# Layer 3's neighbour slots laid out slot by slot and gathered without the empty ones, with edits of layer 1's order, in a four-layer graph network

## The chip, the cores and the metric

The kernel runs on one core of a Trainium2 chip. The metric is the device time of one execution, in microseconds; the numbers of one profiled execution come from the hardware profiler. PE is the matrix engine, DVE the vector engine, ACT the scalar engine, POOL the GpSimd engine, which also issues the indirect DMAs (gathers and scatters of rows by index), and SP the engine that issues most plain DMAs.

## The reference

There are N = 2708 nodes with D = 128 features, and an adjacency matrix of 2708 x 2708 float32 in which about 17 entries a row are not zero (the diagonal is always there). Four layers follow one another, each of the form x = layernorm(x + f(x, adj)):

```
layer 0: f = (adj^T x) / column sums of adj
layer 1: s = x Wa^T, d = x Wb^T;  agg[i] = sum_j adj[i,j] * gelu(s[i] + d[j] + b)
         f = layernorm(gelu([x, agg] U^T + c) + x)
layer 2: h = adj (x W) + b;  f = leaky_relu(batchnorm over nodes (h))
layer 3: for each of 4 heads: x1 = x w1, x2 = x w2
         score[i,j] = exp(8 tanh((leaky_relu(x1[i] + x2[j]) . a) / 8)) * adj[i,j]
         out = leaky_relu((score / row sum) x Wlin^T);  f = concat(heads) w
```

## The kernel before, in words

The adjacency is used as lists. In layer 0 the kernel loads the rows in 22 blocks of 128 nodes. PE makes the column sums and adj^T x (L453), POOL clears the diagonal (L443, an affine select a block) and DVE extracts the positions and values of the non-zero entries (L478 to L521, the extraction of a block). Nodes are then ranked by the number of their neighbours, in two groups (the first SPLIT = 13 blocks and the other 9), and the lists are scattered to memory in that order. `caps` holds, for each block and each 32 nodes, how many neighbours the written tables allow (QUARTERS); where data exceed them a flag sends the program to a dense path, which doesn't run here. Before the extraction there is a little set-up of index patterns by DVE (L700 to L716) from three POOL iotas (L693 to L697). The `caps` memsets (L415) are written ahead of them.

In layer 1 each block of 128 ranked nodes takes its neighbours slot by slot: one gather per slot from `d_dram` (L263, tile msg) into a ring, issued by `gather_spaced`, which puts three short `pause` memsets (L280) on POOL behind every fourth gather. DVE adds the own term `s_ps` (made by PE at L924 to L927 from x_s), ACT does the gelu, DVE weighs and sums (L938, `parts`), PE forms the update (L968 to L979), a normalisation follows, and PE transposes the result (L997) for its row write to `x2_dram`. Other work is put beside the blocks: `layer2(k)`, a gather of 128 rows of the transposed adjacency (`at_rows`) into a ring and one set of matrix products into six standing accumulators (L1076, with a column sum at L1067); lists for layer 3 (L675); and the 13 gathers `x2_first` of layer 2's rows from `x2_dram[0]`, which need all 13 row writes of the first group. A tile scheduler orders the instructions of each engine from the order of writing and its own estimate. Layer 3 is written with a manual order on PE, DVE, ACT and POOL.

In layer 2 the rest of the batch normalisation is done, and for each node a row of 644 floats is written to `t2_dram` (its x2 terms of four heads, its features and padding). Tables for layer 3 (`masks`, iotas at L1170 and L1172) are built in between.

In layer 3 the nodes stand in 24 blocks, `BLOCKS3`, given as (g, j): a chunk holds g nodes with c = 128 // g slots each, e = g c rows, and one index a row. Four chunks make a quad, one from each quarter of the block, j quads a block, 100 quads in all:

```
BLOCKS3 = [
    *[(4, 8), (5, 6), (6, 5), (6, 5), (6, 5), (7, 4), (7, 4), (7, 4), (8, 4), (8, 4), (8, 4)],
    *[(9, 3), (9, 3), (10, 3)],
    *[(4, 3), (5, 5), (6, 4), (6, 5), (7, 3), (7, 4), (8, 4), (8, 4), (9, 3), (10, 3)],
]
```

 `fetch(i)` issues the four gathers of a quad (L263, tile g) into a set of the pool `got`, which rotates over GOT = 9 sets. PE's `repeated` adds up the own terms of the chunk's nodes, and for two chunks the gathered rows (L1463, L1469, tile z); DVE adds the own terms for the other two (L1663), takes leaky relu times a (`scores` L1479, `products` L1487); ACT sums the products over the features (L1495); PE divides out sums and forms the weighted sum of the gathered features (L1540, tile po_s). DVE wrote sums and products into the set of the gathered rows itself. The closing work of a quad is queued and done some quads later. Output rows are scattered from POOL (L284). POOL's order in layer 3 is fetch by fetch with the pauses between, so that the next fetch is issued as soon as a set is free.

Of the kernel before, what the change touches and what calls it, by code (L numbers as in the profile page):

```python
# [9 lines left out]
FP = mybir.dt.float32  # L10
AF = mybir.ActivationFunctionType
ALU = mybir.AluOpType
# [46 lines left out]
]  # L59
KINDS = sorted({g for g, _ in BLOCKS3})  # L60
# [29 lines left out]
GOT = 9  # L90
# [4 lines left out]
def gnn_resnorm_kernel(  # L95
# [155 lines left out]
    wrong3 = keep.tile([P, NB3], FP, name="wrong3")  # L251
# [116 lines left out]
    with ExitStack() as layer:  # L368
# [44 lines left out]
        for b in range(NBLK):  # L413
            for q, most in enumerate(QUARTERS[b]):
                nc.gpsimd.memset(caps[32 * q : 32 * q + 32, b : b + 1], float(most))  # L415
# [52 lines left out]
        def extract(b, rows):  # L468
# [21 lines left out]
            junk = small.tile([P, CAND], FP, name="junk_c")  # L490
# [171 lines left out]
        def spread(b, po, c0):  # L662

            g, j = BLOCKS3[b]
            c, q = P // g, 4 * j
            e = g * c
            for i, k0 in enumerate((0, SLOTS)):
                part = mine.tile([P, g, c], FP, name=f"spread{g}", tag="spread", bufs=2)
                nc.vector.tensor_tensor(
                    part,  # L670
                    lists3[:, b % 6, k0 : k0 + c].unsqueeze(1).to_broadcast((P, g, c)),
                    of_row[g].unsqueeze(2).to_broadcast((P, g, c)),
                    ALU.mult,
                )
                nc.tensor.matmul(  # L675
                    po[0:e, c0 + i * q : c0 + (i + 1) * q],
                    lhsT=part.rearrange("p g c -> p (g c)"),
                    rhs=of_chunk[g][:, 0:j, :].rearrange("p j r -> p (j r)"),
                    start=True, stop=True,
                )  # L680
            at = slice(CHUNK3[b], CHUNK3[b + 1])
            nc.vector.tensor_copy(val3[0:e, at], po[0:e, c0 : c0 + q])
            nc.vector.tensor_copy(idx3[0:e, at], po[0:e, c0 + q : c0 + 2 * q])
            nc.vector.tensor_copy(to3[:, b : b + 1], node3[:, b, 1:2])
            n, bad = 4 * g * j, wrong3[:, b : b + 1]
            nc.vector.tensor_scalar(bad[0:n], node3[0:n, b, 0:1], float(c - 1), None, ALU.is_gt)
            nc.vector.scalar_tensor_tensor(
                bad[0:n], node3[0:n, b, 0:1], 1.0, bad[0:n], ALU.is_lt, ALU.add
            )
# [14 lines left out]
        of_row, of_chunk = {}, {}  # L704
# [48 lines left out]
        nc.scalar.dma_start(w2_l2, l2_w)  # L753
        for b in range(SPLIT):
# [164 lines left out]
        def messages(b, x_s, three):  # L919
# [7 lines left out]
            nc.tensor.matmul(  # L927
                s_ps[0:n], lhsT=ones[0:1, 0:n], rhs=msgb[0:1, :], start=False, stop=True
            )
            parts = mine.tile([P, 2, D], FP, name="parts")  # L930
# [161 lines left out]
        for i, b in enumerate(TURNS):  # L1092
# [9 lines left out]
            x_st, agg = messages(b, x_s, three)  # L1102
# [22 lines left out]
            if i >= 11:  # L1125
                for k in range(2 * (i - 11), min(i, 2 * (i - 10))):
                    layer2(k)
            if i > SPLIT:
                if i == SPLIT + 1:
                    x2_first = late.tile([P, SPLIT, D], FP, name="x2_first", tag="late")  # L1130
                for b in range(2 * (i - SPLIT - 1), min(SPLIT, 2 * (i - SPLIT))):
# [26 lines left out]
    with ExitStack() as layer:  # L1158
# [6 lines left out]
        def masks(g):  # L1165
# [4 lines left out]
            nc.gpsimd.iota(row_of, pattern=[[1, g], [0, c]], base=0, channel_multiplier=0)  # L1170
            start = small.tile([P, g], I32, name=f"start{g}", tag="start", bufs=2)
            nc.gpsimd.iota(start, pattern=[[-c, g]], base=0, channel_multiplier=1)  # L1172
# [16 lines left out]
            after = small.tile([P, g], FP, name=f"after{g}", tag="after", bufs=2)  # L1189
            count = small.tile([P, 1], FP, name="count", bufs=2)  # L1190
            nc.vector.tensor_scalar(
                after, start, 0.0, None, ALU.is_ge, ALU.add, accum_out=count
            )
            mask[g] = ready.tile([P, g], FP, name=f"mask{g}")
            nc.vector.scalar_tensor_tensor(
                mask[g], start, float(c), after, ALU.is_lt, ALU.mult
# [157 lines left out]
    with ExitStack() as layer:  # L1354
        work = layer.enter_context(tc.tile_pool(name="s3", bufs=1, reuse_waits="tile"))
        mine = layer.enter_context(tc.tile_pool(name="s3_mine", bufs=2, reuse_waits="tile"))
        got = layer.enter_context(tc.tile_pool(name="s3_got", bufs=GOT, reuse_waits="tile"))
# [117 lines left out]
        def scores(e, r, z, a, g4, sc):  # L1475

            for hd in range(HEADS):
                part_of = slice(hd * D, (hd + 1) * D)
                nc.vector.scalar_tensor_tensor(  # L1479
                    g4[0:e, r, part_of], z[0:e, part_of], 0.0, a[0:e, part_of],  # L1480
# [3 lines left out]
        def products(e, g4):  # L1484

            z = g4[0:e, 0:2, 0:HD]
# [4 lines left out]
        def sums_of_products(e, g4, sc, chunks):  # L1491
            for r in chunks:
                for hd in range(HEADS):
                    product = g4[0:e, r, hd * D : (hd + 1) * D]
# [139 lines left out]

        def fetch(i):
            b, j = quads[i]
            e = BLOCKS3[b][0] * (P // BLOCKS3[b][0])
            g4 = got.tile([P, 4, RW], FP, name="g4")
            for r in range(4):
                ch = CHUNK3[b] + 4 * j + r  # L1640
                gather_spaced(g4[0:e, r, :], t2_dram, idx3[0:e, ch : ch + 1])
# [4 lines left out]
        for i, (b, j) in enumerate(quads):  # L1646
# [11 lines left out]
            if i + 1 < len(quads):  # L1658
# [3 lines left out]
            z, a_row = g4[0:e, 0:2, 0:HD], a_99.rearrange("p h d -> p (h d)")  # L1662
            nc.vector.tensor_tensor(z, z, z2[0:e], ALU.add)  # L1663
            nc.vector.scalar_tensor_tensor(
                g4[0:e, 2, 0:HD], zs[0][0:e], 0.0, a_row[0:e], ALU.max, ALU.mult
            )
            scores(e, 3, zs[1], a_row, g4, sc4[:, 3, :])
            step()
            sums_of_products(e, g4, sc4, (2,))
# [4 lines left out]
            products(e, g4)  # L1674
            step()
            sums_of_products(e, g4, sc4, (0, 1))
# [531 lines left out]
```

## Time and profile before

| | us |
|---|---|
| median of 3 runs (lowest to highest) | 1655.01 (1653.0 to 1659.47) |
| the profiled execution | 1660.39 |
| its span | 1658.7 |
| mean granted TensorE clock | 0.755 |

In the lines shown below, a group line gives the source line, the engine, the operation, out<-in, the count, then busy time and mean duration in ns, and behind the second bar the idle time just before these instructions with what ended most of it. A line of the windows gives start and end, the length, the busy time of PE, of its weight loads (PEld), of DVE, ACT and POOL, each with its count, the granted clock, the share of the DMA engines and GB/s. A line of the waits gives the engine, the tile and line that waited, what ended the wait, the sum, the count and the longest. A line of the timeline gives start, duration, engine, line, operation and, in brackets, the idle time before it and what ended it. The stages by window: extraction to 208, layer 1 to about 863, layer 2 to 959, layer 3's quads to 1620, and the last blocks' closing to 1659.

### The profile page before, as it was taken

What the parts mean: (1) busy time and instruction counts of PE and PEld (TensorE: products, weight loads), DVE (VectorE), ACT (ScalarE), POOL (GpSimd) and SP (SyncE); (2) the same over time, 40 slices, a digit from 0 to 9 for tenths busy, and PEclk for the clock granted to TensorE, in tenths of its full rate; (3) what the DMA queues carried; (4) which work ended last, traced back from release to release, by engine and by line L of the source; (5) the groups of instructions that cost most, each with busy time, mean ns of one, the idle gap of its engine ahead of it and who ended that gap; (6) DMA issues with size and microseconds to landing.
All of it is one profiled execution on the core that took longest, in us unless ns stands there. A gap on an engine that the chain in (4) does not pass through costs nothing. (4 is left out here: it accounts for less than half of the span.)

```text
span 1658.7 us, 23258 instructions
## 1 busy us (share of the span) xinstructions
PE 1164.1 (70%) x5179; PEld 735.5 (44%) x5179; DVE 1093.4 (66%) x4560; ACT 811.9 (49%) x3491; POOL 1045.7 (63%) x1656
## 2 busy tenths in 40 slices
PE   7976434566248667353576778988889788898985
PEld 6976323445136433131333324544444445454444
DVE  6999767888435452264465555877768777587874
ACT  2638467755134210021122545776658666576763
POOL 2001487777776626777762577777777777777772
PEclk9998555555555578676566877999889999788996
DMA  8633367879546744811111576777677676676761
GB/s 277 260 135 132 90 171 226 240 213 259 135 103 174 252 172 153 314 52 48 41 42 35 202 204 189 200 212 204 190 202 219 192 199 187 191 208 188 216 190 39
DMA packets 163651, 288.42 MB, mean 174 GB/s; under 512 B 46786, under 2 KB 118514, under 8 KB 156401
## 3 DMA queue, kind: packets, MB, share of 16 engines
q0 software_dynamic: 60208, 189.68, 39.4%
q1 hardware_dynamic: 98053, 93.97, 18.4%
q10 hardware_dynamic: 5240, 3.18, 0.8%
q8 instruction: 44, 0.72, 0.2%
q14 instruction: 106, 0.87, 0.2%
HBM read 241.22 MB, written 45.45 MB: 173 GB/s over the span
## 5 line engine op out<-in xcount | busy, mean ns | idle before, releaser
L263 POOL DMA_INDIRECT g<-t_dram,idx x400 | 400.0, 1000 | 149.0 <-issue 105.7
L263 POOL DMA_INDIRECT msg<-d_dram,idx x368 | 347.9, 945 | 132.6 <-issue 78.7
L1495 ACT ACTIVATE g<-g 126x128 f32<-126x128 f32 (+3 forms) x1200 | 352.9, 297 | 65.7 <-DVE g L1487 25.7
L1469 PE MATMUL z<-g,ident 126*126 126x512 f32 (+3 forms) x400 | 245.4, 734 | 69.6 <-DMA g<-t_dram,idx 60.2
L1495 ACT ACTIVATION_READ_ACCUMULATOR g<-g 126x1 f32 (+3 forms) x1200 | 226.0, 188 | 3.6 <-issue 3.3
L1029 PE MATMUL pt_a<-ident,rows 128*128 128x128 f32 (+2 forms) x475 | 119.5, 411 | 118.8 <-ACT at_sb L1034 62.4
L1469 PEld LDWEIGHTS z<-g,ident 126*126 126x126 f32 (+3 forms) x400 | 73.8, 213 | 229.0 <-DMA g<-t_dram,idx 151.7
L1463 PE MATMUL z<-x,copies 32*126 32x512 f32 (+3 forms) x800 | 160.8, 686 | 7.8 <-DVE g L1663 4.8
L280 POOL MEMSET pause<- 1x200 int8 x591 | 150.5, 255 | 20.7
L453 PE MATMUL acc<-x_nat,rows 128*128 128x129 f32 (+3 forms) x1012 | 132.2, 293 | 30.5 <-DMA rows<-in_adj_dram 19.4
L1029 PEld LDWEIGHTS pt_a<-ident,rows 128*128 128x128 f32 (+2 forms) x475 | 84.4, 210 | 146.8 <-ACT at_sb L1034 76.1
L1663 DVE TENSOR_TENSOR g<-g,z 126x1024 f32<-126x1024 f32 (+3 forms) x100 | 121.7, 1217 | 41.8 <-PE z L1463 21.5
L1076 PE MATMUL acc<-at_rows,x_nat 128*128 128x512 f32 (+2 forms) x264 | 139.4, 676 | 13.4 <-DMA at_rows<-at_dram,perm 13.4
L453 PEld LDWEIGHTS acc<-x_nat,rows 128*128 128x128 f32 (+2 forms) x1012 | 126.1, 202 | 36.2 <-DMA rows<-in_adj_dram 20.7
L1487 DVE SCALAR_TENSOR_TENSOR g<-g,a_ps 126x1024 f32<-126x1024 f32 (+3 forms) x100 | 121.2, 1212 | 0.0
L938 DVE SCALAR_TENSOR_TENSOR own<-msg,ls,own 128x128 f32<-128x128 f32 (+1 forms) x302 | 105.4, 349 | 20.6 <-ACT msg L957 10.5
L957 ACT ACTIVATE msg<-msg 128x896 f32<-128x896 f32 (+4 forms) x55 | 50.4, 916 | 137.7 <-DVE msg L954 68.6
L1479 DVE SCALAR_TENSOR_TENSOR g<-z,a 126x128 f32<-126x128 f32 (+3 forms) x400 | 91.9, 285 | 35.0 <-PE z L1469 31.0
L1540 PEld LDWEIGHTS po_s<-wm,g 126*128 126x128 f32 (+3 forms) x800 | 105.3, 208 | 17.4 <-issue 12.3
L954 DVE TENSOR_TENSOR msg<-msg,own 128x896 f32<-128x896 f32 (+4 forms) x55 | 57.4, 1043 | 79.8 <-DMA msg<-d_dram,idx 76.1
L1540 PE MATMUL po_s<-wm,g 126*128 126x24 f32 (+6 forms) x800 | 103.4, 280 | 1.4 <-DVE wm L1527 0.9
L478 DVE FIND_INDEX8 ci<-cv,rows 128x8 uint32<-128x247 f32 (+2 forms) x242 | 98.5, 407 | 0.0
(319 smaller groups left out, 2058.2 us busy)
## 6 DMA issues: line engine op xcount, KB each, us to landing
rows<-in_adj_dram SPq DMA_DIRECT2D x34, 1354.0 KB
at_dram<-at_sb SPq DMA_DIRECT2D x105, 256.0 KB
t_dram<-t_row SPq DMA_DIRECT2D x10, 644.0 KB
g<-t_dram,idx POOLq DMA_INDIRECT x400
msg<-d_dram,idx POOLq DMA_INDIRECT x368
x_s<-dx_dram SPq DMA_DIRECT2D x21, 128.0 KB
at_dram<-at_sb SPq DMA_DIRECT2D x21, 64.0 KB
x_dram<-x_n SPq DMA_DIRECT2D x21, 64.0 KB
```

Of the source, the lines that this page charges most:

```text
L263: return nc.gpsimd.indirect_dma_start(out=dst, out_offset=None, in_=table[0 : min(N, table.shape[0]), :], in_offset=bass.IndirectOffsetOnA ...
L280: did = nc.gpsimd.memset(pause, 0)
L453: nc.tensor.matmul(accs0[k][0:m, c0 : c0 + f1 - f0], lhsT=rows[0:n, j0 : j0 + m], rhs=x_nat[0:n, b, f0:f1], start=k not in started, stop=( ...
L938: nc.vector.scalar_tensor_tensor(to, m, v, last, ALU.mult, ALU.add)
L1029: nc.tensor.transpose(pt[0:m, j, 0:n], rows[0:n, c0 : c0 + m], ident[0:n, 0:n])
L1076: nc.tensor.matmul(accs2[c][:, 0:cw], lhsT=xw[0:n, b, :], rhs=at[0:n, c0 : c0 + cw], start=(k == 0), stop=(k == NBLK - 1),)
L1463: nc.tensor.matmul(z2[0:e, r, :] if r < 2 else zs[r - 2][0:e], lhsT=copies[g][rows, j, :], rhs=own[b][1][rows, :], start=True, stop=r < 2, ...
L1469: nc.tensor.matmul(zs[r - 2][0:e], lhsT=ident[0:e, 0:e], rhs=g4[0:e, r, 0:HD], start=False, stop=True, skip_group_check=True,)
L1487: nc.vector.scalar_tensor_tensor(z, z, 0.0, a_ps[0:e].unsqueeze(1).to_broadcast((e, 2, HD)), ALU.max, ALU.mult)
L1495: nc.scalar.activation(product, product, AF.Identity, accum_out=sc[0:e, r, hd : hd + 1])
L1540: nc.tensor.matmul(po[:, p0 * HEADS : (p0 + g) * HEADS], lhsT=g4s[i][0:e, r, HD : HD + D], rhs=wm[0:e, 4 * i + r, :, :], start=True, stop= ...
L1663: nc.vector.tensor_tensor(z, z, z2[0:e], ALU.add)
```

## The change

- `QUARTERS3` says, for each block of layer 3 and each of the four chunks of a quad, how many slots the fullest node may have. The rows of a chunk are laid slot by slot (all g nodes' first slot, then all second ones) in place of node by node, in `spread`, the index patterns and the `masks`. So the empty slots lie at the end, and `fetch` gathers only the first m = g * QUARTERS3[b][r] rows from quad 8 on; the first eight quads gather all e rows, so that every set has been filled once.
- The lists are held against these caps (`caps3`, `wrong3`, `of_block`). The memsets of `caps` are written after the iotas, in fewer pieces, and those of `caps3` with them. In POOL's order the first affine select then comes before these memsets (46 of 128 rows, 81 of 32) and the second one after them.
- Layer 3's sums and products go into a tile of their own, `made`, with two buffers.
- GOT is 8, as eight tiles given out once. A gather then waits for its index and for PE, where the first gather of a quad waited for DVE, DMA, PE and ACT.
- In layer 1 the 13 `x2_first` gathers are written from turn 16 on, three a turn, where it was turn 14 and two. Two `layer2` sets are put behind the own term of the next block on PE, where they stood at the end of a turn; the last block takes three (18, 19 and 20), and set 21 comes at the end as before.

```diff
 ]
+QUARTERS3 = [
+    (31, 26, 25, 24), (23, 22, 22, 22), (21, 21, 21, 20), (20, 20, 20, 19),
+    (19, 19, 19, 19), (18, 18, 18, 18), (18, 17, 17, 17), (17, 17, 16, 16),
+    (16, 16, 16, 16), (15, 15, 15, 15), (14, 14, 14, 14), (14, 13, 13, 13),
+    (13, 12, 12, 12), (11, 11, 10, 9), (30, 26, 24, 24), (23, 23, 22, 21),
+    (21, 21, 20, 20), (20, 19, 19, 19), (18, 18, 18, 18), (17, 17, 17, 16),
+    (16, 16, 16, 15), (15, 15, 14, 14), (14, 13, 13, 13), (12, 12, 11, 9),
+]
 KINDS = sorted({g for g, _ in BLOCKS3})
...
 TOGETHER3 = [(0, 4), (4, 8), (8, 12), (12, 16), (16, 20), (20, 23), (23, 24)]
-GOT = 9
+GOT = 8
 LEAD3 = 5
...
 caps = work.tile([P, NBLK], FP, name="caps")
-for b in range(NBLK):
-    for q, most in enumerate(QUARTERS[b]):
-        nc.gpsimd.memset(caps[32 * q : 32 * q + 32, b : b + 1], float(most))
+caps3 = work.tile([P, NB3], FP, name="caps3")
...
 for i, k0 in enumerate((0, SLOTS)):
-    part = mine.tile([P, g, c], FP, name=f"spread{g}", tag="spread", bufs=2)
+    part = mine.tile([P, c, g], FP, name=f"spread{g}", tag="spread", bufs=2)
     nc.vector.tensor_tensor(
         part,
-        lists3[:, b % 6, k0 : k0 + c].unsqueeze(1).to_broadcast((P, g, c)),
-        of_row[g].unsqueeze(2).to_broadcast((P, g, c)),
+        lists3[:, b % 6, k0 : k0 + c].unsqueeze(2).to_broadcast((P, c, g)),
+        of_row[g].unsqueeze(1).to_broadcast((P, c, g)),
         ALU.mult,
...
 po[0:e, c0 + i * q : c0 + (i + 1) * q],
-lhsT=part.rearrange("p g c -> p (g c)"),
+lhsT=part.rearrange("p c g -> p (c g)"),
 rhs=of_chunk[g][:, 0:j, :].rearrange("p j r -> p (j r)"),
...
 nc.vector.tensor_copy(to3[:, b : b + 1], node3[:, b, 1:2])
-n, bad = 4 * g * j, wrong3[:, b : b + 1]
-nc.vector.tensor_scalar(bad[0:n], node3[0:n, b, 0:1], float(c - 1), None, ALU.is_gt)
+n = 4 * g * j
+nc.vector.tensor_scalar(
+    wrong3[0:n, b : b + 1], node3[0:n, b, 0:1], 1.0, None, ALU.is_lt
+)
 nc.vector.scalar_tensor_tensor(
-    bad[0:n], node3[0:n, b, 0:1], 1.0, bad[0:n], ALU.is_lt, ALU.add
+    wrong3[:, NB3 + b : NB3 + b + 1], lists3[:, b % 6, 2 * SLOTS : 2 * SLOTS + 1],
+    caps3[:, b : b + 1], of_block[g * j], ALU.is_gt, ALU.mult,
 )
...
 nc.vector.tensor_copy(in32, row_i)
-of_row, of_chunk = {}, {}
+of_row, of_chunk, of_block = {}, {}, {}
+spans = sorted({g * j for g, j in BLOCKS3})
+of_blocks3 = work.tile([P, len(spans)], FP, name="of_blocks3")
+for i, e in enumerate(spans):
+    of_block[e] = of_blocks3[:, i : i + 1]
+    nc.vector.tensor_scalar(of_block[e], in32, float(e), None, ALU.is_lt)
 for g in KINDS:
...
 nc.scalar.dma_start(w2_l2, l2_w)
+for b in range(NBLK):
+    for q, most in enumerate(QUARTERS[b]):
+        if not q or most != QUARTERS[b][0]:
+            at = slice(32 * q, 32 * q + 32) if q else slice(0, P)
+            nc.gpsimd.memset(caps[at, b : b + 1], float(most))
+for b in range(NB3):
+    for q, most in enumerate(QUARTERS3[b]):
+        if not q or most != QUARTERS3[b][0]:
+            at = slice(32 * q, 32 * q + 32) if q else slice(0, P)
+            nc.gpsimd.memset(caps3[at, b : b + 1], float(most - 1))
 for b in range(SPLIT):
...
-def messages(b, x_s, three):
+def messages(b, x_s, three, beside):
     n, kk = BLOCKS[b][1], CAPS[b]
...
 nc.tensor.matmul(s_ps[0:n], lhsT=x_st[:, 0:n], rhs=ws_t, start=True, stop=False)
-nc.tensor.matmul(
+term = nc.tensor.matmul(
     s_ps[0:n], lhsT=ones[0:1, 0:n], rhs=msgb[0:1, :], start=False, stop=True
 )
+for k in beside:
+    with tc.issue_after(term.ins):
+        layer2(k)
 parts = mine.tile([P, 2, D], FP, name="parts")
...
     load3(b3)
-x_st, agg = messages(b, x_s, three)
+x_st, agg = messages(
+    b, x_s, three,
+    range(2 * (i - 12), 2 * (i - 11) if i + 1 < NBLK else i) if i > 11 else (),
+)
 for _ in range(2 if i < 1 else 1):
...
     accs2.extend(banks("acc2_"))
-if i >= 11:
-    for k in range(2 * (i - 11), min(i, 2 * (i - 10))):
-        layer2(k)
-if i > SPLIT:
-    if i == SPLIT + 1:
+if i > SPLIT + 2:
+    if i == SPLIT + 3:
         x2_first = late.tile([P, SPLIT, D], FP, name="x2_first", tag="late")
-    for b in range(2 * (i - SPLIT - 1), min(SPLIT, 2 * (i - SPLIT))):
+    for b in range(3 * (i - SPLIT - 3), min(SPLIT, 3 * (i - SPLIT - 2))):
         gather_spaced(x2_first[:, b, :], x2_dram[0], rank[:, b : b + 1])
...
 row_of = small.tile([P, e], I32, name=f"row_of{g}", tag="row_of", bufs=2)
-nc.gpsimd.iota(row_of, pattern=[[1, g], [0, c]], base=0, channel_multiplier=0)
-start = small.tile([P, g], I32, name=f"start{g}", tag="start", bufs=2)
-nc.gpsimd.iota(start, pattern=[[-c, g]], base=0, channel_multiplier=1)
+nc.gpsimd.iota(row_of, pattern=[[0, c], [1, g]], base=0, channel_multiplier=0)
+apart = small.tile([P, c, g], I32, name=f"apart{g}", tag="apart", bufs=2)
+nc.gpsimd.iota(apart, pattern=[[-g, c], [-1, g]], base=0, channel_multiplier=1)
 first = small.tile([P, 8], FP, name="first", bufs=2)
...
 nc.vector.tensor_scalar(alike[g], row_of, 1.0, place_of, ALU.add, ALU.is_equal)
-after = small.tile([P, g], FP, name=f"after{g}", tag="after", bufs=2)
-count = small.tile([P, 1], FP, name="count", bufs=2)
+here = small.tile([P, c, g], FP, name=f"here{g}", tag="here", bufs=2)
 nc.vector.tensor_scalar(
-    after, start, 0.0, None, ALU.is_ge, ALU.add, accum_out=count
+    here.rearrange("p c g -> p (c g)"), apart.rearrange("p c g -> p (c g)"),
+    0.0, None, ALU.is_equal,
 )
 mask[g] = ready.tile([P, g], FP, name=f"mask{g}")
+nc.vector.tensor_reduce(mask[g], here.rearrange("p c g -> p g c"), AX.X, ALU.add)
+count = small.tile([P, 1], FP, name="count", bufs=2)
 nc.vector.scalar_tensor_tensor(
-    mask[g], start, float(c), after, ALU.is_lt, ALU.mult
+    each, jrow[:, 0:g], 1.0, mask[g], ALU.add, ALU.mult, accum_out=count
 )
...
 mine = layer.enter_context(tc.tile_pool(name="s3_mine", bufs=2, reuse_waits="tile"))
-got = layer.enter_context(tc.tile_pool(name="s3_got", bufs=GOT, reuse_waits="tile"))
+got = layer.enter_context(tc.tile_pool(name="s3_got", bufs=1, reuse_waits="tile"))
 small = layer.enter_context(tc.tile_pool(name="s3_small", bufs=3, reuse_waits="tile"))
...
-def scores(e, r, z, a, g4, sc):
+def scores(e, r, z, a, made, sc):
...
 nc.vector.scalar_tensor_tensor(
-    g4[0:e, r, part_of], z[0:e, part_of], 0.0, a[0:e, part_of],
+    made[0:e, r, part_of], z[0:e, part_of], 0.0, a[0:e, part_of],
     ALU.max, ALU.mult, accum_out=sc[0:e, hd : hd + 1],
...
-def products(e, g4):
+def products(e, made):
-    z = g4[0:e, 0:2, 0:HD]
+    z = made[0:e, 0:2, :]
     nc.vector.scalar_tensor_tensor(
...
-def sums_of_products(e, g4, sc, chunks):
+def sums_of_products(e, made, sc, chunks):
     for r in chunks:
         for hd in range(HEADS):
-            product = g4[0:e, r, hd * D : (hd + 1) * D]
+            product = made[0:e, r, hd * D : (hd + 1) * D]
             nc.scalar.activation(
...
+sets = [got.tile([P, 4, RW], FP, name=f"g4_{i}") for i in range(GOT)]
+
 def fetch(i):
...
 e = BLOCKS3[b][0] * (P // BLOCKS3[b][0])
-g4 = got.tile([P, 4, RW], FP, name="g4")
+g4 = sets[i % GOT]
 for r in range(4):
     ch = CHUNK3[b] + 4 * j + r
-    gather_spaced(g4[0:e, r, :], t2_dram, idx3[0:e, ch : ch + 1])
+    m = BLOCKS3[b][0] * QUARTERS3[b][r] if i >= GOT else e
+    gather_spaced(g4[0:m, r, :], t2_dram, idx3[0:m, ch : ch + 1])
 gathered[i] = g4
...
         leave()
-z, a_row = g4[0:e, 0:2, 0:HD], a_99.rearrange("p h d -> p (h d)")
-nc.vector.tensor_tensor(z, z, z2[0:e], ALU.add)
+made = small.tile([P, 4, HD], FP, name="made", bufs=2)
+a_row = a_99.rearrange("p h d -> p (h d)")
+nc.vector.tensor_tensor(made[0:e, 0:2, :], g4[0:e, 0:2, 0:HD], z2[0:e], ALU.add)
 nc.vector.scalar_tensor_tensor(
-    g4[0:e, 2, 0:HD], zs[0][0:e], 0.0, a_row[0:e], ALU.max, ALU.mult
+    made[0:e, 2, :], zs[0][0:e], 0.0, a_row[0:e], ALU.max, ALU.mult
 )
-scores(e, 3, zs[1], a_row, g4, sc4[:, 3, :])
+scores(e, 3, zs[1], a_row, made, sc4[:, 3, :])
 step()
-sums_of_products(e, g4, sc4, (2,))
+sums_of_products(e, made, sc4, (2,))
 if i + 1 < len(quads):
...
     ahead = repeated(*quads[i + 1], gathered[i + 1])
-products(e, g4)
+products(e, made)
 step()
-sums_of_products(e, g4, sc4, (0, 1))
+sums_of_products(e, made, sc4, (0, 1))
 step()
```

More of the change, by code (lines that the diff above doesn't have):

```diff
@@ L250, in gnn_resnorm_kernel @@
     to3 = keep.tile([P, NB3], I32, name="to3")
-    wrong3 = keep.tile([P, NB3], FP, name="wrong3")
+    wrong3 = keep.tile([P, 2 * NB3], FP, name="wrong3")
     nc.gpsimd.memset(wrong3, 0.0)
@@ L489, in extract @@
             kb = small.tile([P, CAND], FP, name="kb")
-            junk = small.tile([P, CAND], FP, name="junk_c")
+            junk = small.tile([P, CAND], FP, name="junk_c", bufs=1)
             nc.vector.tensor_tensor(ka[0:n], cv[0:n], scales[0:n], ALU.mult)
```

## The prediction

> **What bounds the kernel now.** I read the page first, then the span cut into stages (start and end, length, busy time of each engine, granted clock, share of the DMA engines, GB/s), then the waits by engine, then timelines of the places that the diff touches.
>
> ```profile
> span 1658.7 us, 23258 instructions
> PE 1164.1 (70%) x5179; PEld 735.5 (44%) x5179; DVE 1093.4 (66%) x4560; ACT 811.9 (49%) x3491; POOL 1045.7 (63%) x1656
> L263 POOL DMA_INDIRECT g<-t_dram,idx x400 | 400.0, 1000 | 149.0 <-issue 105.7
> L263 POOL DMA_INDIRECT msg<-d_dram,idx x368 | 347.9, 945 | 132.6 <-issue 78.7
> ```
>
> ```profile
> 0.00:208.00 208.00, 150.25 (x1086) 140.30 (x1087) 180.79 (x984) 101.53 (x161) 44.20 (x178) 0.83 0.52 179
> ...
> 863.00:900.00 37.00, 29.65 (x64) 14.12 (x62) 18.08 (x95) 5.99 (x17) 8.06 (x19) 0.68 0.12 34
> ...
> 959.00:1620.00 661.00, 574.52 (x2583) 308.16 (x2586) 480.82 (x1582) 436.08 (x2672) 493.57 (x716) 0.89 0.71 201
> ```
>
> Three bounds follow one another. To 208 us it is DVE (180.8 busy of 208). From 208 to 863 and from 959 to 1620 it is POOL issuing gathers: in layer 3, 400 gathers (400.0) with idle before them (149.0), three pauses a quad (0.88 us, about 90 in all) and 18 output scatters fill the 661 us. PE there waits for the data, not the other way round:
>
> ```profile
> PEld z L1469 <- DMA g<-t_dram,idx: 151.7, 116, 4.6
> ...
> POOL x_first L263 <- issue: 38.1, 13, 36.1
> ```
>
> So layer 3 is priced by what one gather costs POOL, not by bytes. In layer 1 the gathers fetch 20 to 128 rows, median 945 ns whatever the count. In layer 3 the price goes with how the rows divide. The trace's packets lie on the largest number of DMA engines, up to 16, that divides the row count: 128 rows on 16, 120 on 15, 126 on 14, 125 on 5. Medians: 947, 981, 984 and 1197 ns. A quad of 125 rows, then one of 128 (start, duration, idle before):
>
> ```profile
> 1005.03 1.22 POOL L263 DMA_INDIRECT g<-t_dram,idx  x1 [0.20 <-issue]
> 1006.55 1.19 POOL L263 DMA_INDIRECT g<-t_dram,idx  x1 [0.30 <-issue]
> ...
> 1227.45 0.98 POOL L263 DMA_INDIRECT g<-t_dram,idx  x1 [0.56 <-PE po_s L1540]
> 1228.73 0.96 POOL L263 DMA_INDIRECT g<-t_dram,idx  x1 [0.30 <-issue]
> ```
>
> **The change, part by part** (us; sum against the profiled execution, 1660.4, which is 5.4 above the median 1655.0).
>
> *Memsets behind the iotas: −2.*
>
> ```profile
> 3.14 11.27 POOL L415 MEMSET caps<- 32x1 f32 x88
> ...
> 14.84 0.24 DVE L700 TENSOR_SCALAR more<-four_i 128x4 f32<-128x4 int32 x1 [11.42 <-POOL four_i L697]
> ...
> 20.39 0.73 DVE L483 MAX8 cv<-rows 128x8 f32<-128x247 f32 x2
> ```
>
> DVE's 5.6 us of set-up can now run at 3.4, and block 0's extraction, which needs PE's start at 11.04 and the first affine select, at about 12.5 instead of 20.4. But 127 memsets (46 of 128 rows, 81 of 32) stand before the second select; at 11.27/88 = 0.128 each, 16.3 us. Block 1's extraction, 31.4 before (11.0 after block 0's start), then waits until 12.5 + 16.3 = 28.8 and a select of 0.3. From there DVE has no gap above 0.4 to 170, so the rest moves up by 2 (bounds 0 and −8, the second if wider memsets cost next to nothing). The eight added DVE set-up operations (about 0.2 each) lie in the wait for x.
>
> *x2_first later: −10.* POOL is in order, and its first x2_first gather waits for block 12's row write:
>
> ```profile
> 592.35 0.25 POOL L280 MEMSET pause<- 1x200 int8 x1
> 628.74 0.95 POOL L263 DMA_INDIRECT x_first<-x_dram,rank  x1 [36.13 <-issue]
> ```
>
> In the written order the first gather moves from POOL's 394th place to its 403rd only: one at_rows and four message gathers come ahead of it, about 6.8 us. Block 12's write follows PE's x_n transpose (626.52). On PE 4.65 layer-2 sets stood between 594.7 and it, now 4, at about 4.8 each: 3 earlier. Stall 36 to 26, gain 10. Bounds: 7 (PE gains nothing) and 36 (all of it).
>
> *Layer-2 sets with the next block's own term: +6.* In mid-layer the six sets that ran together from 628 to 674, with PE waits for at_rows of 4.6 and 7.2, become two a block, and POOL's later waits (2.7, 1.7 and 2.3 between 692 and 725) may go: −3. Later at_rows gathers wait for ring slots that PE frees later; bounds −7 and +8, the sizes of the waits seen. At the end:
>
> ```profile
> 866.31 7.19 PE L1076 MATMUL acc<-at_rows,x_nat 20*128 20x512 f32 x8
> 875.33 0.45 PE L997 MATMUL tail<-ident,x_n 128*128 128x128 f32 x1 [1.82 <-DVE x_n L350]
> 877.28 1.22 PE L968 MATMUL tail<-ident,parts 128*128 128x128 f32 x4 [0.36 <-ACT x_nat L1002]
> ...
> 881.09 7.18 PE L1076 MATMUL acc<-at_rows,x_nat 128*128 128x512 f32 x10
> 888.62 0.31 PE L997 MATMUL tail<-ident,x_n 128*128 128x128 f32 x1 [0.34 <-DVE less L1231]
> ```
>
> Before, set 20 runs while DVE normalises the last block, hidden. After, sets 18, 19 and 20 all stand ahead of the last block's parts: from 866 three of 7.2 put it at about 888 instead of 877.3, and only set 21 is left behind it. +9 (bounds 0, if the clock or late messages cover it, and +12).
>
> *Masks: +1.* Seven iotas of e elements in place of g (0.27 against 0.13 in the rows of L1170 and L1172) and one more DVE operation a kind, on the way to layer 3's first gather.
>
> *Rows left out in layer 3: +7.* From quad 8 on, gathers have 90 to 128 rows, 47,208 in all for 50,460. Now 124 gathers of 128 rows, 208 of 126, 44 of 125, 24 of 120 cost about 400. After, 102 go on 16 engines (947), 81 on 15 (981), 61 are of 126 (986): 236.3. The other 156 have row counts that no gather of this size here has: 117 and 104 divide by 13, 108 by 12, 110 by 11, 100 by 10, 119 by 7, 114 by 6, 115 by 5. At 986 each the sum is 390 (−10); at 1201, the row nearest to 115, 424 (+24). A straight line in the engine count between 986 at 14 and 1201 at 5 gives 410 (+10); if the cost goes with the rows of each list too (25 a list at 125 rows, 19 at 114) it is about 405. I take +7. The Trainium skill, "DMA: Bandwidth & Descriptors", section "Why a DMA increments its semaphore by 16 and not by 1", says that a DMA is given the largest number of engines up to 16 that divides its slowest dimension; the packets here agree (125 rows on 5). It speaks against 114, 115 and 119, though it names no issue cost.
>
> *Waits in layer 3: −6.* A quad's first gather waited for four things, now two (or three): 0.54 to 0.66 idle before it. Layer 1's gathers after the same three pauses, with two waits, show 0.445: −0.09 on some 70 quads. Added PE waits on the other three are hidden: in layer 1 a satisfied wait between gathers leaves the idle at 0.305. Bounds 0 and −20.
>
> *Eight sets, own product tiles: 0.* Against the trace before, PE's last read of quad q ends before POOL comes to quad q+8 in every case, by 0.5 at least (quad 2), mostly 10 to 25. The adds and products keep count and shapes (121.7 and 121.2 in all); PE frees a set alone.
>
> Sum: −2 −10 −3 +9 +1 +7 −6 = −4; 1656 on the profiled execution, 1651 on the median.
>
> **The rivals.**
> - *Ill-divided row counts cost full price* (slower). If lists on 5 to 13 engines all cost the 125-row 1.2 us, layer 3 is +24 in place of +7: 1668. It turns the sign when those 156 gathers average above about 1.12. For it: 1197 against 984 for one row less. Against: only one bad divisor has been seen.
> - *Divisors matter little* (faster): the 156 at 0.99, −17: 1634. For it: 14 and 15 engines cost only 35 ns more than 16, and layer 1's 20-row gathers cost 945.
> - *The stall goes altogether* (faster): if block 12 is written by 599, another −24: 1627. Against: own(12)'s transpose starts at 594 after a DVE wait that the change leaves.
> - *Layer 3 follows bytes* (faster): −6.4% of 400 is −26: about 1620. Against: 20 and 128 rows at 945.
> - *The later own sets only trade places* and stall and tail cancel: that is the forecast's own middle.
>
> **How the numbers follow.** Within 0.5% is 1646.7 to 1663.3, about what a measurement tells from no change. Forecast 0.46, of which 0.08 falls below 1646.7; full price 0.27; divisors little 0.17; stall gone 0.06; bytes 0.04. Faster 0.08 + 0.17 + 0.06 + 0.04 = 0.35, same 0.38, slower 0.27. Own range of the forecast: 1643 to 1662. To hold 8 in 10 the range takes in 1634 and 1668 with a few us each way: 1631 to 1672.
>
> **What would show it.** Right: the x_first wait about 26; layer 3's gathers about 407 in all, those of 115 rows about 1.2 and of 114 in between; the idle before a quad's first near 0.45; the last x_n transpose later after the last message gather (25.8 before) by 9. Wrong: a gather group above 420 or below 393; waits of POOL for PE on g, which would make eight sets too few; a second select well before 28.

## The result and the profile after

The changed kernel takes 1645.05 us (median, 1639.78 to 1648.16) where the kernel before takes 1655.01: a ratio of 0.9933, 95% interval 0.9907 to 0.9959. Repeated beside other kernels on another chip it gave 0.9954 (0.9935 to 0.9973). So it is faster by some 0.5 to 0.7%, 6.5 to 10 us; 1651 was forecast.

The two profiled executions lie further apart than the medians (1660.4 lies just above the slowest other run of its kernel, 1639.8 is the fastest of its own), so differences of single stages from this pair are good to a few us only. The page of the changed kernel:

```profile
span 1638.1 us, 23273 instructions
PE 1142.1 (70%) x5179; PEld 725.7 (44%) x5179; DVE 1099.3 (67%) x4575; ACT 810.6 (49%) x3491; POOL 1052.0 (64%) x1694
...
L271 POOL DMA_INDIRECT g<-t_dram,idx x400 | 402.9, 1007 | 143.5 <-issue 89.1
L271 POOL DMA_INDIRECT msg<-d_dram,idx x368 | 347.3, 944 | 127.6 <-issue 77.0
```

On the page the engines' shares are within one point of those before. Layer 3's gathers cost POOL a little more (402.9 for 400.0) with a little less idle before them (143.5 for 149.0), although 6.4% fewer rows come in. The start, in the timelines of POOL and then of DVE (start, duration, idle before):

```profile
2.52 0.44 POOL L410 MEMSET scales<- 128x8 f32 x11
...
11.79 0.80 POOL L772 MEMSET caps<- 128x1 f32 x22
12.52 0.86 POOL L777 MEMSET caps<- 128x1 f32 x24
13.43 4.67 POOL L772 MEMSET caps<- 32x1 f32 x40
18.14 4.76 POOL L777 MEMSET caps<- 32x1 f32 x40
22.97 0.29 POOL L449 TENSOR_SCALAR_AFFINE_SELECT rows<-rows 128x128 f32<-128x128 f32 x1
```

```profile
23.30 0.74 DVE L489 MAX8 cv<-rows 128x8 f32<-128x247 f32 x2 [0.32 <-POOL rows L449]
```

The 46 memsets of 128 rows took 1.7 us, not 5.9; only those of 32 rows cost 0.12 each (there are 80 of them, 40 a table, not 81). So the second select came at 23.0, just when DVE was through with block 0, and block 1's extraction starts at 23.3 where it was 31.4.

In the middle of layer 1, where POOL stood once at the first x_first gather, its timeline shows two waits now: one at an at_rows gather that needs a ring slot from PE, and a shorter one for block 12's write:

```profile
587.82 0.95 POOL L271 DMA_INDIRECT at_rows<-at_dram,perm  x1 [7.30 <-PE acc L1103]
...
607.95 0.95 POOL L271 DMA_INDIRECT x_first<-x_dram,rank  x1 [13.79 <-DMA x_dram<-x_n]
```

And the end of layer 1 on PE: sets 18, 19 and 20 (L1094 and L1103) all stand before the last parts (L995).

```profile
835.92 4.79 PE L1103 MATMUL acc<-at_rows,x_nat 128*128 128x148 f32 x12
...
840.89 5.68 PE L1103 MATMUL acc<-at_rows,x_nat 20*128 20x148 f32 x12
846.78 0.45 PE L1024 MATMUL tail<-ident,x_n 128*128 128x128 f32 x1 [0.22 <-DVE x_n L358]
...
849.19 7.61 PE L1103 MATMUL acc<-at_rows,x_nat 128*128 128x148 f32 x12
856.64 0.61 PE L995 MATMUL tail<-ident,parts 128*128 128x128 f32 x4
...
866.23 0.45 PE L1024 MATMUL tail<-ident,x_n 128*128 128x128 f32 x1 [7.31 <-DVE less L1260]
```

Cut at five instructions of the timelines (the first and the last message gather on POOL, the last x_n transpose on PE, the first and the last gather of layer 3 on POOL), the spans stand as follows, in us. The first two rows are the pair of the prediction; the next four ran on one chip, the four after them on another, the last four on a third.

| kernel | start | messages | tail | layer 2 | layer 3's gathers | rest | span |
|---|---|---|---|---|---|---|---|
| before | 211.2 | 651.6 | 25.8 | 70.4 | 659.9 | 39.8 | 1658.7 |
| changed | 203.2 | 629.7 | 33.3 | 73.9 | 656.2 | 41.7 | 1638.1 |
| before again | 211.0 | 642.9 | 26.4 | 66.9 | 660.2 | 40.7 | 1648.1 |
| changed again | 203.3 | 629.9 | 37.6 | 76.4 | 656.1 | 42.2 | 1645.4 |
| layer 1's part alone | 211.2 | 635.4 | 33.2 | 69.8 | 659.3 | 41.1 | 1650.0 |
| changed, old caps memsets | 212.7 | 632.3 | 34.5 | 76.2 | 657.1 | 41.7 | 1654.5 |
| changed, layer 1 as before | 203.2 | 634.8 | 25.2 | 70.6 | 655.8 | 43.7 | 1633.4 |
| changed, all rows | 203.2 | 630.8 | 29.7 | 73.2 | 653.6 | 40.7 | 1631.3 |
| changed, divisible rows | 203.1 | 627.9 | 27.0 | 72.7 | 637.5 | 37.6 | 1605.8 |
| changed, memsets written first | 203.1 | 632.1 | 27.1 | 73.0 | 657.1 | 42.6 | 1635.1 |
| changed, 7 buffers of apart | 203.4 | 627.0 | 26.9 | 72.8 | 657.1 | 41.0 | 1628.1 |
| changed, set 20 last | 203.6 | 629.6 | 23.0 | 73.4 | 656.1 | 41.0 | 1626.7 |
| changed, rotating sets, all rows | 203.3 | 632.7 | 27.3 | 72.9 | 654.7 | 41.9 | 1632.9 |
| all together | 203.4 | 621.4 | 23.2 | 67.2 | 638.4 | 37.8 | 1591.5 |

Each row is a single trace. The start and layer 3's gathers agree between chips within 1 us; messages, tail and layer 2 differ by up to some 10 between traces of the same kernel (the kernel with the memsets written first runs as the changed one does, and is counted as such). So there only rows of one chip are held together, and small differences even of those prove little by themselves.

### The profile page after: what moved, and what is told of

The parts are those of the page before. It is cut to its first block, busy times and chain, and to the rows that moved or that the text cites. A ratio compares the mean times of both kernels' runs of the same rounds, so it can differ in the third digit from the quotient of the medians.

```text
span 1638.1 us, 23273 instructions
## 1 busy us (share of the span) xinstructions
PE 1142.1 (70%) x5179; PEld 725.7 (44%) x5179; DVE 1099.3 (67%) x4575; ACT 810.6 (49%) x3491; POOL 1052.0 (64%) x1694
## 5 line engine op out<-in xcount | busy, mean ns | idle before, releaser
L271 POOL DMA_INDIRECT g<-t_dram,idx x400 | 402.9, 1007 | 143.5 <-issue 89.1
L1524 ACT ACTIVATE made<-made 126x128 f32<-126x128 f32 (+3 forms) x1200 | 352.8, 297 | 70.9 <-DVE made L1697 31.4
L1524 ACT ACTIVATION_READ_ACCUMULATOR made<-made 126x1 f32 (+3 forms) x1200 | 225.8, 188 | 0.0
L1056 PE MATMUL pt_a<-ident,rows 128*128 128x128 f32 (+2 forms) x475 | 114.6, 399 | 119.9 <-ACT at_sb L1061 62.4
L1492 PE MATMUL z<-x,copies 32*126 32x512 f32 (+3 forms) x800 | 151.6, 676 | 8.2 <-issue 3.2
L1696 DVE TENSOR_TENSOR made<-g,z 126x1024 f32<-126x1024 f32 (+3 forms) x100 | 121.6, 1216 | 42.5 <-PE z L1492 14.9
L459 PE MATMUL acc<-x_nat,rows 128*128 128x129 f32 (+3 forms) x1012 | 130.1, 290 | 24.6 <-DMA rows<-in_adj_dram 13.9
L1103 PE MATMUL acc<-at_rows,x_nat 128*128 128x512 f32 (+2 forms) x264 | 131.2, 654 | 0.0
L1516 DVE SCALAR_TENSOR_TENSOR made<-made,a_ps 126x1024 f32<-126x1024 f32 (+3 forms) x100 | 121.3, 1213 | 0.0
L1508 DVE SCALAR_TENSOR_TENSOR made<-z,a 126x128 f32<-126x128 f32 (+3 forms) x400 | 91.9, 285 | 36.4 <-PE z L1498 32.7
```

Of the source, the lines that this page charges most:

```text
L271: return nc.gpsimd.indirect_dma_start(out=dst, out_offset=None, in_=table[0 : min(N, table.shape[0]), :], in_offset=bass.IndirectOffsetOnA ...
L459: nc.tensor.matmul(accs0[k][0:m, c0 : c0 + f1 - f0], lhsT=rows[0:n, j0 : j0 + m], rhs=x_nat[0:n, b, f0:f1], start=k not in started, stop=( ...
L1056: nc.tensor.transpose(pt[0:m, j, 0:n], rows[0:n, c0 : c0 + m], ident[0:n, 0:n])
L1103: nc.tensor.matmul(accs2[c][:, 0:cw], lhsT=xw[0:n, b, :], rhs=at[0:n, c0 : c0 + cw], start=(k == 0), stop=(k == NBLK - 1),)
L1492: nc.tensor.matmul(z2[0:e, r, :] if r < 2 else zs[r - 2][0:e], lhsT=copies[g][rows, j, :], rhs=own[b][1][rows, :], start=True, stop=r < 2, ...
L1516: nc.vector.scalar_tensor_tensor(z, z, 0.0, a_ps[0:e].unsqueeze(1).to_broadcast((e, 2, HD)), ALU.max, ALU.mult)
```

## The experiments

The first theory, from the two traces: the gain is the start (−8) and layer 1's shorter stall, less a longer tail; layer 3 is about even, since a gather's price goes with the divisor of its row count. The rival: the gain is layer 3's, through the rows left out.

### Layer 1 as before

```diff
-            for k in beside:
-                with tc.issue_after(term.ins):
-                    layer2(k)
...
+            if i >= 11:
+                for k in range(2 * (i - 11), min(i, 2 * (i - 10))):
+                    layer2(k)
-            if i > SPLIT + 2:
+            if i > SPLIT:
...
```

> The changed kernel with layer 1's part undone: x2_first gathers written from turn 14, two a turn, and the layer-2 sets at the end of a turn, as in the kernel before. Theory (the gain is layer 1's stall and the earlier start, layer 3 is about even): from the first message gather to the last x_n transpose 677 us again in place of 663, the first x_first gather waits more than 30 us again, and the time is about 14 above the changed kernel's 1645, 1657 to 1661. Rival (the gain is layer 3's, through the rows left out): about 1645, layer 1's share is lost in other waits.

Measured: 1634.75, 0.9936 of the kernel before on that chip (0.9916 to 0.9956). The wait of the first x_first gather was 26.8, and from the first message gather to the last x_n transpose it took 660.0; a kernel of the same group that runs as the changed one does (memsets written first, below) took 659.2 and 1631.36. So the theory's 14 us for layer 1 fell: with the new order the messages are shorter (632.1 for 634.8) and tail and layer 2 longer (27.1 for 25.2, 73.0 for 70.6).

### Layer 1's part alone, on the kernel before

The same edit the other way round on the kernel before.

> The kernel before with layer 1's part alone (x2_first gathers from turn 16, three a turn; layer-2 sets behind the next own term). Theory after the first runs (the shorter stall is given back by the longer tail and by layer 2): message gathers about 15 shorter, tail from the last message gather to the last x_n transpose about 7 longer and layer 2 some 3 longer, time 0.996 to 1.000 of the kernel before. Rival (the prediction's first sum without its tail): gain of 13 or more, 0.992 or less.

Measured: 0.9996 (0.9981 to 1.0012), no difference. The stall fell from 30.0 in the second trace of the kernel before to 13.9, but POOL then waited 14.3 in all at at_rows gathers that need a ring slot (3.6 before). Against that trace, messages −7.5 (about −15 was expected), tail +6.8, layer 2 +2.9. The waits of POOL in this kernel:

```profile
POOL x_first L263 <- issue: 16.0, 13, 13.9
```

The revised theory holds in the time, the tail and layer 2: the part gives back at the end of layer 1 what it gains in the middle. The stall is not shorter because block 12 was written earlier: PE's x_n transpose for it began 408.2 us after the first message gather, 406.0 in the second trace of the kernel before. POOL came to the x_first gather later instead, with five more gathers (about 1.26 each) and the ring wait behind it.

### The memsets of the caps

First all of them were written ahead of the iotas.

> The changed kernel with the memsets of both caps tables back ahead of the iotas (the same 127 memsets, only their place). Theory (the start is a chain of POOL's iotas, DVE's set-up and a DVE-bound stage): block 0's extraction starts at about 20 in place of 11.9, the first message gather at about 211 in place of 203, time 8 later, about 1653. Rival (later waits of layer 0 take the shift in): first message gather within 2 us of 203, time about 1645.

This did not undo the start: the scheduler put the 46 quick memsets in front and left the 80 slow ones behind the first select, block 0's extraction began at 12.2, and the time was 1631.36, 0.9913 (0.9888 to 0.9938). The run says nothing on the theory; it serves as the changed kernel of its group. Then the first table's memsets were put back just as before:

```diff
+        for b in range(NBLK):
+            for q, most in enumerate(QUARTERS[b]):
+                nc.gpsimd.memset(caps[32 * q : 32 * q + 32, b : b + 1], float(most))
         caps3 = work.tile([P, NB3], FP, name="caps3")
...
-        for b in range(NBLK):
-            for q, most in enumerate(QUARTERS[b]):
-                if not q or most != QUARTERS[b][0]:
...
```

> The changed kernel with the 88 memsets of caps in 32-row pieces ahead of the iotas, exactly as in the kernel before; the new table's memsets stay behind the first select. Theory (the start is a chain of POOL's iotas, DVE's set-up and a DVE-bound stage): first extraction at 20, the first message gather at about 211 to 214 in place of 203, time 8 to 11 above the changed kernel, 0.998 to 1.000 of the kernel before. Rival (later waits of layer 0 take the shift in): first message gather within 2 of 203, same time as the changed kernel.

Measured: 1655.73 beside 1646.9 for the changed kernel and 1653.42 for the kernel before: 1.0016 (1.0000 to 1.0032). The first message gather came at 212.7, and block 0's extraction started as late as in the kernel before, in DVE's timeline:

```profile
21.78 0.73 DVE L492 MAX8 cv<-rows 128x8 f32<-128x247 f32 x2
```

With this one edit undone the change is no faster, so the start is worth 8.8 us, more than the whole gain of 6.5 on that chip.

> The changed kernel, unchanged, beside the next two runs. Both theories: 0.991 to 0.995 of the kernel before; first message gather at 203, fetch of quad 0 at about 937, last gather of layer 3 some 656 later.

> The kernel before, unchanged, for a second trace of it. Theory: the first x_first gather waits about 36 us again and the stages (start to first message gather, messages, tail, layer 2, layer 3) are within 3 us of the first trace. Rival (the stall and the loads before it vary from run to run by as much as the change moves them): the wait differs by over 5 us.

The second traces: the changed kernel at 0.9954, start and layer 3 as expected; quad 0's fetch came at 947, 10 later, through a tail and a layer 2 longer than in its first trace (37.6 for 33.3, 76.4 for 73.9). In the kernel before, the x_first wait was 30.0, not 36.1, and messages took 642.9, not 651.6: here the rival held, and a part of the first pair's 22 us of messages was the spread between runs.

### The rows

```diff
-                m = BLOCKS3[b][0] * QUARTERS3[b][r] if i >= GOT else e
+                m = e
```

> The changed kernel with all e rows gathered in every quad, so that the empty slots are fetched again; layout, own product tiles and eight fixed sets stay. Theory (POOL's issue sets layer 3 and a gather's price goes with the divisor of its row count, not with the rows): layer 3's gathers 400 busy in place of 403, the first idle about the same, time within 4 us of 1645. Rival (layer 3 follows rows or bytes): 7% more rows from quad 8 on cost 20 to 26 us, about 1668, and PE waits longer for data.

Measured: 1629.35, 0.9893 (0.9863 to 0.9924). All rows gathered again and the kernel is not slower (1631.36 with rows left out): layer 3's gathers took 653.6, 3.5 less than with fewer rows (657.1). Bytes are out as the bound. The gathers' line of this kernel:

```profile
L271 POOL DMA_INDIRECT g<-t_dram,idx x400 | 399.0, 997 | 144.6 <-issue 79.4
```

Then the row counts were raised to those that divide well:

```diff
+        def issue_cost(rows):
+            lists = max(k for k in range(1, 17) if rows % k == 0)
+            return (16 - lists) * ((rows // lists) // 2)
...
                 m = BLOCKS3[b][0] * QUARTERS3[b][r] if i >= GOT else e
+                m = min(range(m, e + 1), key=lambda rows: (issue_cost(rows), rows))
```

> The changed kernel with each short gather's row count raised to the cheapest one not above e by the price seen (116 of 368 gathers with 114, 115, 117 or 119 rows fetch 120, 110 to 100 fetch 112, 31 with 120 rows fetch 128 where the chunk has them): 48,102 rows in place of 47,208. Theory (price by divisor): layer 3's gathers fall from 403 busy to about 386 and the time by 16 to 20, to 1625 to 1630. Rival (rows count): no faster, 1645 to 1653, since more rows are fetched.

Measured: 1610.48, 0.9797 (0.9772 to 0.9823), 21 us below the changed kernel of its group, with 894 more rows. Quad 8, with 5 nodes a chunk, in POOL's timeline: first the changed kernel (115, 110, 110 and 110 rows), then this one (120, 112, 112, 112).

```profile
986.89 1.19 POOL L271 DMA_INDIRECT g<-t_dram,idx  x1 [0.59 <-PE z L1492]
988.38 0.99 POOL L271 DMA_INDIRECT g<-t_dram,idx  x1 [0.30 <-issue]
989.68 1.00 POOL L271 DMA_INDIRECT g<-t_dram,idx  x1 [0.30 <-PE z L1498]
990.98 0.99 POOL L271 DMA_INDIRECT g<-t_dram,idx  x1 [0.30 <-PE po_s L1569]
```

```profile
977.42 1.00 POOL L271 DMA_INDIRECT g<-t_dram,idx  x1 [0.52 <-PE po_s L1569]
978.73 0.96 POOL L271 DMA_INDIRECT g<-t_dram,idx  x1 [0.30 <-PE z L1492]
979.99 0.92 POOL L271 DMA_INDIRECT g<-t_dram,idx  x1 [0.30 <-issue]
981.22 0.92 POOL L271 DMA_INDIRECT g<-t_dram,idx  x1 [0.30 <-issue]
```

And the gathers' lines, of the kernel with the memsets written first and of this one:

```profile
L271 POOL DMA_INDIRECT g<-t_dram,idx x400 | 403.8, 1009 | 143.5 <-issue 80.0
```

```profile
L271 POOL DMA_INDIRECT g<-t_dram,idx x400 | 386.4, 966 | 141.2 <-issue 84.7
```

The gathers' busy time falls by 17.4 (403.8 to 386.4) and the stretch by 19.6 (657.1 to 637.5). The price by divisor is shown, and more rows made the kernel faster.

### The waits of a quad's first gather

```diff
-            g4 = sets[i % GOT]
+            g4 = got.tile([P, 4, RW], FP, name="g4")
...
-                m = BLOCKS3[b][0] * QUARTERS3[b][r] if i >= GOT else e
+                m = e
```

> The changed kernel with the pool's eight rotating sets in place of eight fixed ones, and all e rows gathered (the fixed sets are what lets a gather leave stale rows behind). To be held against the run with all rows and fixed sets. Theory (the idle before a quad's first gather goes with the number of waits that the gather carries): about 525 ns idle before a quad's first gather in place of 473, layer 3's loop some 5 longer. Rival (the products' own tile made the difference): idle about 470 again.

From a single execution: the mean idle before a quad's first gather was 481 ns, against 473 with fixed sets and all rows and 526 before. So the fixed sets make 8 ns of the 53, and the rival is nearer. The other 45 are put down to the products' own tile, after which DVE and ACT no longer write or read the set; that is by elimination, since no run takes the tile away alone. Time 1634.71 (span 1632.9).

### Layer 2's tables and the last sets

```diff
-            apart = small.tile([P, c, g], I32, name=f"apart{g}", tag="apart", bufs=2)
+            apart = small.tile([P, c, g], I32, name=f"apart{g}", tag="apart", bufs=7)
```

> The changed kernel with seven buffers in place of two for the new masks tile apart. Theory (POOL, in order, is held at an apart iota until DVE has read the tile two kinds earlier, and the x_second gathers behind it come late): the last x_second gather 17 after the last x_n transpose in place of 22.5, layer 2 (last x_n transpose to quad 0's first gather) 5 to 6 shorter, time 0.990 to 0.993 of the kernel before. Rival (the later scatters or the weights end last anyway): layer 2 within 1.5 of the changed kernel's, time about 0.995.

Measured: 0.9935 (0.9916 to 0.9955). The last x_second gather came 19.4 after the last x_n transpose (23.6 and 23.9 in two kernels of its group), and DVE's first t_row, the rows that layer 3 gathers, 33.6 after it (34.7 and 35.1). But layer 2 took 72.8 (72.9 and 73.4): the rival. Most of the gain was lost between the first t_row and quad 0's gather (39.2 for 38.2 and 38.3).

```diff
-                range(2 * (i - 12), 2 * (i - 11) if i + 1 < NBLK else i) if i > 11 else (),
+                range(2 * (i - 12), 2 * (i - 11) if i + 1 < NBLK else 20) if i > 11 else (),
...
-        layer2(NBLK - 1)
+        for k in range(20, NBLK):
+            layer2(k)
```

> The changed kernel with only sets 18 and 19 beside the last block's own term; set 20 is put behind its update in the writing, and the scheduler then places it between the last parts and their update on PE. Theory (the three sets ahead of the last block's parts are the longer tail): from the last message gather to the last x_n transpose about 30 in place of 33 to 38, time 3 to 7 lower, 0.991 to 0.994. Rival (the set only changes its place within the same chain): tail within 2 of the changed kernel's, time about 0.995.

Measured: 0.9909 (0.9874 to 0.9943), tail 23.0 against 26.9 and 27.3 of two kernels of its group that keep the three sets together. The tail is 4 shorter, as the theory asked, though all three lie below the lengths it named; by time alone the interval is too wide to tell it from the changed kernel.

### All together

> All that the runs point to, in one kernel: the changed kernel with the row counts raised to the cheap ones, x2_first gathers written from turn 18 (four a turn), set 20 behind the last update, seven apart buffers. Theory (the parts add up, each with its own place): x_first wait under 5, layer 3's gathers 386 busy, layer 2 about 68 to 70, 0.966 to 0.974 of the kernel before. Rival (layer 1's parts trade places and only the row counts count): 0.977 to 0.983.

Measured: 1595.97, 0.9715 (0.9688 to 0.9742): 46 us below the kernel before, in the theory's range. In the waits of POOL the stall is gone, and the group has the cheap row counts:

```profile
POOL x_first L271 <- issue: 2.4, 13, 0.5
```

```profile
L271 POOL DMA_INDIRECT g<-t_dram,idx x400 | 386.9, 967 | 141.6 <-issue 79.0
```

Messages are 5.6 to 11.3 shorter than in the other three kernels of its group, tail 23.2, layer 2 67.2. Layer 2 is 5.6 to 6.2 shorter here. The largest part, 3.4 to 3.7, is that the last layer-2 set on PE, set 21, ends 6.5 after the last x_n transpose began, where it was 9.9 to 10.2. First the changed kernel with set 20 last, then this one:

```profile
858.58 7.80 PE L1103 MATMUL acc<-at_rows,x_nat 128*128 128x148 f32 x12
```

```profile
849.82 4.79 PE L1103 MATMUL acc<-at_rows,x_nat 128*128 128x148 f32 x12
```

The granted clock over this set was 1.00 here and 0.61 to 0.63 in the other three kernels of the group. Which of the edits brought that was not isolated; x2_first's later place is made in this kernel alone.

## Why the prediction was right

The time lies in the range and on the predicted side, with −0.5 to −0.7% where −0.25% was forecast, but not all steps held. The range, 1631 to 1672, takes in no change as well, so the steps say more than the total. Of the signs named, gathers of 115 rows at about 1.2 and a later last x_n transpose came; the second select well before 28 (it came at 23.0), named as a sign of being wrong, came too. Step by step (predicted, measured):

- *Memsets behind the iotas: −2, measured −8 to −9.* The mechanism was right, a term was mis-sized: the 46 memsets of 128 rows were priced at 0.128 like those of 32 rows. They take 0.036. The trace of before had the row that says so, eleven memsets of 128x8 in 0.44, and it was nearer in shape than the 88 of 32x1. The bound of −8 was named. On the chip where this step was undone it is the whole gain: the ratio is 1.0016. On the next chip the kernel that runs as the changed one (memsets written first) gained 13.9; the kernel before has no trace there, so what else took part is open.
- *x2_first later: −10, and the middle of layer 1: −3.* Alone, messages fell by 7.5 beside a second trace of before. The five gathers that moved ahead were counted rightly; that PE would have block 12 ready 3 us earlier is not borne out. Its transpose moved from 406.0 after the first message gather to 408.2 alone and to 402.2 in the changed kernel; on the next chip it stood at 401.5 with layer 1 as before and at 407.2 with the new order. The stall went to 14, less than the 26 forecast, but much of it came back as a wait at an at_rows gather for a ring slot that PE frees later (7.3 in the changed kernel, 11.6 with layer 1's part alone), the cost that the bounds of +8 stood for.
- *Sets ahead of the last parts: +9.* Measured +6.8 alone, +7.5 in the first pair and +11.2 in the second, only about 2 on another chip. The order on PE is as forecast (sets 18 to 20, then parts). The sum for layer 1 was −4; measured 0 (0.9996).
- *Masks: +1, measured +3.4.* A mis-sized term. From the end of set 21 on PE to DVE's first t_row it took 21.4 to 21.5 in all three traces with the old masks and 24.8 to 24.9 in all nine with the new ones and two apart buffers. Seven buffers make it 23.3, so POOL's wait at the new apart iotas, which was not in the step, is 1.5 of it; the other 1.9 stay open. Layer 2 as a whole grew by 3.5 in the first pair and 9.5 in the second. Of that, 2.2 to 2.3 lie in set 21 and what stands just ahead of it: the set took 6.4 at a granted clock of 0.74 to 0.75 in place of 4.79 at 1.00. With layer 1's part alone it took 6.4 too, but 6.5 in the changed kernel with layer 1 as before, so which edit does this is open. The rest, from the first t_row to quad 0's gather, lay between 37.4 and 42.8 in an order that follows no edit.
- *Rows left out: +7, measured +2.6.* The gathers' busy time rose from 400.0 and 400.3 to 402.9 and 402.6. Medians after: 997 ns at 110 rows, 1117 at 114, 1182 at 115, 988 at 117, 1095 at 119. Both rivals on the price fail: it is neither 1.2 us for all nor 0.99; the 156 gathers average 1.07. The second of the two estimates, in which the rows of each list count as well as the number of lists (+5), was the better one; taking the mean with the straight line was part of the error, and the rest is that it too was high. The run with divisible counts turned the price into 21 us. The Trainium skill, "DMA: Bandwidth & Descriptors", section "Why a DMA increments its semaphore by 16 and not by 1", gives the divisor rule for the number of engines. The durations here go with that number (947 at 128 rows on 16, 1182 at 115 on 5). The packets agree with it too: cut by the rule, with two table rows to a packet and an odd row alone, layer 3's gathers make 23,664 pairs and 3,132 single rows before and 22,389 and 2,430 after, and so many of 5152 and 2576 bytes are in the traces.
- *Waits: −6.* The mean idle before a quad's first gather fell from 526 to 465 ns, 6.0 over 99 quads, as forecast. The typical idle fell less far than said (median 594 to 514, not 445), and the fixed sets made little of it; the products' own tile is the likely rest.
- *Eight sets: 0.* Held: no idle of POOL before these gathers that a release by PE ended was above 1.1; layer 3's gathers took 656 for 660, the −6 and +2.6 of the two steps above.

The rival that the stall goes altogether did not come, nor that layer 3 follows bytes (all rows gathered: not slower). One reading against bytes was a little off: 945 ns is the median of all layer 1's gathers, 904 that of the eight with 20 rows. The steps as measured, −8 +0 +3.4 +2.6 −6, make −8, between the −10 and −6.5 of the two chips. That this lies near the forecast −4 is in part luck: the start gained 6 more and the rows cost 4 less than forecast, against 4 less from layer 1 and 2 more for the masks.

## What to carry to other kernels

Where an engine is busy issuing gathers, price a gather by how its row count divides among the DMA engines before leaving rows out; a few rows more can be cheaper, as 120 for 114. A gather moved to a later line of the program moves only as far as the scheduler lets it: look at its place in the engine's order. Work put into a pause in the middle of a stage has left its old place: look at what it now stands in front of at the end.

## What was not expected of the hardware

- A POOL memset of 128 rows and one element takes 36 ns in a row of 22, one of 32 rows 117 ns (40 in 4.67 us).
- The issue time of an indirect gather on POOL with 2576-byte table rows, by row count: 128 rows 947, 112 rows 944, 96 rows 932 ns (16 lists, one for each DMA engine that the rows are dealt to); 120 rows 982 (15); 126 rows 986 (14); 110 rows 997 (11); 119 rows 1095 (7); 114 rows 1117 (6); 115 rows 1182 (5). Below 16 lists, 973 + 1.72 (16 − lists) (half the rows of a list, rounded down) fits the dear ones: 1128 for 114, 1181 for 115, 1097 for 119. It was fitted to these same runs and is too high for smaller counts: 1016 for 110, and 978 for 90, which took 942.
- Two traces of the same kernel differ by up to 9 us in layer 1's messages, 11 in the tail and 4 in layer 2 (between chips, the memsets written first counted as the changed kernel), but by 1 at most in layer 3's issue-bound stretch.
